# Layer 1's two branches combined sequence by sequence inside the experts' stream, and layer 2's small weights loaded during layer 1

## The chip, the core and the metric

The kernel runs on one core of one Trainium2 chip. Each core has five engines that run on their own and wait for each other through semaphores: TensorE (PE, matmuls; PEld is its weight load), VectorE (DVE), ScalarE (ACT), GpSimd (POOL) and SyncE (SP), which here only issues DMAs. Each engine works through its own list of instructions in order. The metric is device time in microseconds of one launch, the median of three runs.

## The reference, cut to what matters

The input x has 8 sequences of 512 tokens with 128 channels. Four layers follow each other, and each has two branches on the same normalized input, which are multiplied and added to x:

```python
xn = _layernorm(x, axis=-1)
s = _L1_attn_ref(xn, Wq, Wk, Wv, Wo)                  # attention branch of layer 1
g = _silu(_L1_ffn_ref(xn, Wg, W1, b1, W2, b2))        # experts' branch of layer 1
x = x + s * g
xn = _layernorm(x, axis=-1)                           # layer 2 starts from here
s = _L2_attn_ref(xn, ...)
g = _silu(_L2_ffn_ref(xn, ...))
x = x + s * g
```

Layer 1's attention has 16 heads of 8 values with a squared score in place of the exponential. Its second branch is a choice of 8 experts, each of which works on up to 1024 tokens that may belong to any sequence. So `s` of a sequence is known when its attention is done, and `g` of any sequence only when the last expert has added its part.

## The kernel before

Tokens lie 128 to a tile row, so a sequence is `JT` = 4 tiles and all of x is `NT` = 32. x stays on the chip in one tile through all layers.

**Layer 1's loop.** `layer1` (L1133) runs over 128 units (sequence b of 8, group of heads g of 4, block of keys kc of 4). For each unit `weights` (L1065) makes the scores on PE and squares them on ACT (L1078), a mask goes over them on VectorE (L1083), and two units later `sums` (L1088) multiplies them with the values (L1097). `group` (L1105) finishes a group of heads, and after the fourth group of a sequence it makes the attention branch `s` for that sequence (L1128, copied out of PSUM at L120 or L122). One step of the generator `side` is taken per unit: `choice_and_experts` (L963) first picks the tokens of each expert and then runs the eight experts between the attention's instructions.

**The experts' output.** Each expert's result `ys` (L1013, L1014 on VectorE) is added to the array `f_d` in DRAM by eight indirect DMAs that GpSimd issues (L1016). Each of them adds, so each waits for the one before it to land; there are 64 in all.

**Between layers 1 and 2.** When the loop is over, `combine` (L176) takes x in four pieces of two sequences: it loads the piece of `f_d` (L184, SyncE), takes its Silu on ScalarE (L188), multiplies by `s` on VectorE (L189) and adds to x on GpSimd (L194). Then `Layer2` loads its two packs of weights, the small one `c2` (1226 KB) and the large one `f2` (2888 KB), both at L126, and `begin(0)` normalizes the first sequence: sums at L1230, mean at L1231, difference at L1232, squares on ScalarE at L1248, sums of squares at L1250, a power on GpSimd at L1240, product at L1234, and then PE transposes the result (L168). `half_s` (L1270) is layer 2's first reader of `f2`.

**What sets the order.** The order of PE's instructions is the order in which the Python code issues them. That of the other engines' instructions is laid down when the program is built, by a planner that goes by durations of its own; the chip keeps to it. A pool's memory is given to the next pool, and the first writer of the new tile then waits for the last users of the old one.

Of the kernel before, what the change touches and what calls it, by code (L numbers as in the profile page):

```python
# [10 lines left out]
F32 = mybir.dt.float32  # L11
# [3 lines left out]
AF = mybir.ActivationFunctionType  # L15
ALU = mybir.AluOpType
# [4 lines left out]
P = 128  # L21
B = 8
T = 512
C = 128
N = B * T
NT = N // P
JT = T // P
# [8 lines left out]
class Pack:  # L36


    def __init__(self):
        self.parts, self.at, self.n = [], {}, 0  # L40
# [32 lines left out]
def bc(ap, axis, n):  # L73

    a = ap.unsqueeze(axis)
    shape = list(a.shape)
    shape[axis] = n
    return a.to_broadcast(shape)


class Kern:
# [80 lines left out]
    def to_features(self, src, dst, nt=NT, scale=None, bias=None):  # L162

        nc = self.nc
        for g in range(0, nt, 4):
# [6 lines left out]
                nc.vector.tensor_scalar(out, flat, scale, bias, ALU.mult, ALU.add)  # L172
            else:
                self.evac(out, flat)

    def combine(self, pool, x, s, f_dram=None, f=None, x_dram=None):  # L176

        nc = self.nc
        G = 8
        for g in range(0, NT, G):  # L180
            sl = slice(g, g + G)
            if f_dram is not None:
                ft = pool.tile([P, G, C], F32, name="cmb_f")
                nc.sync.dma_start(ft, f_dram[g * P : (g + G) * P, :].rearrange("(j p) c -> p j c", p=P))  # L184
            else:
                ft = f[:, sl, :]
            sg = pool.tile([P, G, C], F32, name="cmb_sg")
            nc.scalar.activation(sg, ft, AF.Silu)  # L188
            nc.vector.tensor_tensor(sg, sg, s[:, sl, :], ALU.mult)  # L189
            old = x[:, sl, :]  # L190
            if x_dram is not None:
                old = pool.tile([P, G, C], F32, name="cmb_x")
                nc.sync.dma_start(old, x_dram[:, sl, :])
            nc.gpsimd.tensor_tensor(x[:, sl, :], old, sg, ALU.add)  # L194

    def causal(self, a, n=None, src=None):

# [720 lines left out]
class Layer1:  # L918
# [4 lines left out]


    def __init__(self, k, cp, x, A, at):
        self.k, self.A = k, A
        nc, tc = k.nc, k.tc
        self.xn_d = k.dram.tile([N, C], F32, name="xn1_d")
        self.f_d = k.f1_d
        self.cn = k.load_consts(cp, A["c1"], at, "c1")  # L930
        self.xT = cp.tile([P, N], F32, name="xT1")
        self.s = cp.tile([P, NT, C], F32, name="s1")
        self.idx = cp.tile([P, E1, 8], I32, name="idx1")
        self.gate = cp.tile([P, E1, 8], F32, name="gate1")

        self.va2 = [cp.tile([P, JT, H * 9 + 23], F32, name=f"va1{i}") for i in range(2)]
        for t in self.va2:
            nc.gpsimd.memset(t, 0.0)
            nc.gpsimd.memset(self.by_head(t)[:, :, :, 8:9], 1.0)


        self.ceiling = cp.tile([P, P], F32, name="ceiling1")
        nc.gpsimd.memset(self.ceiling, float(np.finfo(np.float32).max))
        k.causal(self.ceiling)
        self.sending = False
        with tc.tile_pool(name="l1a", bufs=2) as tp, tc.tile_pool(name="l1a1", bufs=1) as tp1:
            xn = tp1.tile([P, NT, C], F32, name="xn1")
            k.layernorm(tp, x, xn, k.eps5)
            for g in range(0, NT, 8):
                nc.sync.dma_start(  # L950
                    self.xn_d[g * P : (g + 8) * P, :].rearrange("(j p) c -> p j c", p=P), xn[:, g : g + 8, :]
                )
            k.to_features(xn, self.xT)
        self.q = {}
# [8 lines left out]
    def choice_and_experts(self):  # L963

        k, nc, cn, A = self.k, self.k.nc, self.cn, self.A
        idx, gate = self.idx, self.gate
        yield from choose1(k, cn, self.xT, idx, gate)
        self.sending = True
        with k.tc.tile_pool(name="l1w", bufs=2) as wp, k.tc.tile_pool(name="l1e", bufs=2) as ep:
            for e in range(E1):  # L970
                w1 = wp.tile([P, FF1], F32, name="w1_1")
                nc.sync.dma_start(w1, A["w1_1"][:, e * FF1 : (e + 1) * FF1])
                w2 = wp.tile([P, 4, C], F32, name="w2_1")
                nc.sync.dma_start(w2.rearrange("p f c -> p (f c)"), A["w2_1"][:, e * 4 * C : (e + 1) * 4 * C])
                xg = ep.tile([P, 8, C], F32, name="xg1")
                for i in range(8):
                    nc.gpsimd.indirect_dma_start(
                        out=xg[:, i, :], out_offset=None, in_=self.xn_d,
                        in_offset=bass.IndirectOffsetOnAxis(ap=idx[:, e, i : i + 1], axis=0),
                    )  # L980
                if e == 0:
                    yield
                    yield
                xgT = ep.tile([P, 2, 512], F32, name="xgT1")
                for hf in range(2):
                    pt = k.pa((P, 4, P))
                    for i in range(4):
                        nc.tensor.transpose(pt[:, i, :], xg[:, hf * 4 + i, :], k.ident)
                    nc.vector.tensor_copy(xgT[:, hf, :], pt.rearrange("p a b -> p (a b)"))
                yield  # L990
                hT = []
                for hf in range(2):
                    hT.append(ep.tile([P, 4, 512], F32, name="hT1"))
                    for f in range(4):
                        ph = k.pa()
                        nc.tensor.matmul(ph, w1[:, f * P : (f + 1) * P], xgT[:, hf, :], start=True, stop=True)
                        nc.scalar.activation(
                            hT[hf][:, f, :], ph, AF.Gelu, bias=cn["b1"][:, e * 4 + f : e * 4 + f + 1]
                        )
                    yield  # L1000
                ys = ep.tile([P, 8, C], F32, name="ys1", bufs=1)
                for hf in range(2):
                    po = k.pa((P, 4, C))
                    for i in range(4):
                        o = slice(i * P, (i + 1) * P)
                        for f in range(4):
                            nc.tensor.matmul(
                                po[:, i, :], hT[hf][:, f, o], w2[:, f, :], start=(f == 0), stop=(f == 3)
                            )
                        if i == 1:  # L1010
                            yield
                    y = ys[:, hf * 4 : hf * 4 + 4, :]
                    nc.vector.tensor_tensor(y, po, bc(cn["b2"][:, e * C : (e + 1) * C], 1, 4), ALU.add)  # L1013
                    nc.vector.tensor_tensor(y, y, bc(gate[:, e, hf * 4 : hf * 4 + 4], 2, C), ALU.mult)  # L1014
                    for i in range(hf * 4, hf * 4 + 4):
                        nc.gpsimd.indirect_dma_start(  # L1016
                            out=self.f_d, out_offset=bass.IndirectOffsetOnAxis(ap=idx[:, e, i : i + 1], axis=0),
                            in_=ys[:, i, :], in_offset=None, compute_op=ALU.add,
                        )
                    yield  # L1020

    def begin(self, b):

# [81 lines left out]
    def group(self, b, g):  # L1105

        k, nc, cn, yp, q = self.k, self.k.nc, self.cn, self.yp, self.q[b]
# [19 lines left out]
        for j in range(JT):  # L1127
            nc.tensor.matmul(ps[:, j, :], sT[:, j * P : (j + 1) * P], cn["Wo"], start=True, stop=True)  # L1128
        k.evac(self.s[:, b * JT : (b + 1) * JT, :], ps)
        yield  # L1130


def layer1(k, x, A, at):  # L1133
    nc, tc = k.nc, k.tc
    with ExitStack() as ctx:
        ctx.enter_context(k.banks("l1p", pu=2, pf=1, pa=3))
        pool = lambda name, bufs=1: ctx.enter_context(tc.tile_pool(name=name, bufs=bufs))
        L = Layer1(k, pool("l1c"), x, A, at)
# [3 lines left out]
        units = [(b, g, kc) for b in range(B) for g in range(4) for kc in range(JT)]  # L1142
        for _ in L.begin(0):
            pass
        side = L.choice_and_experts()
        held = {}
        front = back = iter(())
        for u in range(len(units) + LAG):
            if u < len(units):
                b, g, kc = units[u]  # L1150
# [11 lines left out]
        for _ in chain(back, side):  # L1162
            pass
        work.close()
        k.combine(pool("l1z", 2), x, L.s, f_dram=L.f_d)

# [89 lines left out]
class Layer2(BySequence):  # L1258


    def __init__(self, k, ctx, x, A, at):
        self.k, self.x = k, x
        nc, tc = k.nc, k.tc
        pool = lambda name, bufs=1: ctx.enter_context(tc.tile_pool(name="l2" + name, bufs=bufs))
        cp = pool("c")
        self.cn = cn = k.load_consts(cp, A["c2"], at[0], "c2")
        self.fn = fn = k.load_consts(cp, A["f2"], at[1], "f2")

        self.half_s = cp.tile([P, 4], F32, name="half_s")
# [260 lines left out]

def layer2(k, x, A, at):

    with ExitStack() as ctx:
        ctx.enter_context(k.banks("l2p", pu=2, pf=1, pa=3))
        L = Layer2(k, ctx, x, A, at)
        units = [(b, g, kc) for b in range(B) for g in range(4) for kc in range(JT)]
# [12 lines left out]
        for u in range(len(units) + LAG):  # L1549
            b, n = divmod(u, U)  # L1550
# [11 lines left out]
            if u >= LAG:  # L1562
                wb, g, kc = units[u - LAG]
# [541 lines left out]

PACKS = (pack0, pack1, pack2, pack3)
LAYERS = (layer0, layer1, layer2, layer3)


# [35 lines left out]
```

## Time and profile before

| | |
|---|---|
| median of three runs | 3640.95 us (3640.08 to 3649.79) |
| the profiled execution's own time | 3647.2 us |
| its span in the profile | 3645.5 us |
| mean granted TensorE clock | 0.83 |
| busy over the span | PE 2815.7 us, DVE 2315.1, ACT 1645.2, POOL 743.0 |
| layer 1's loop ends, last `s` copied | at 1444.6 us |
| PE's first instruction of layer 2 | at 1465.0 us |

A row of the timeline is: start in us, length in us, engine, line, operation, output<-input, shapes, count, and in brackets how long the engine sat idle before it and what ended that. A row with a count above 1 merges neighbours. A row of the table of stretches gives for each stretch the busy time of each engine, the granted TensorE clock as a share of full speed (PEclk), the DMA engines' busy share and the rate. All times of the prediction are those of this one profiled execution, which took 6.25 us more than the median of the runs.

### The profile page before, as it was taken

How to read it: one execution, taken by the hardware profiler on the slowest of the kernel's cores; microseconds unless marked ns; L12 is line 12 of the kernel's file. 1: busy time of each engine (PE TensorE's matmuls, PEld its weight loads, DVE VectorE, ACT ScalarE, POOL GpSimd, SP SyncE). 2: the span in 40 equal slices, each digit the busy share in tenths (PEclk: the TensorE clock that was granted, in tenths of full speed). 3: DMA queues.
4: the chain of work that ended last, by engine and by line, in shares of the span. 5: the costliest groups of instructions: out<-in, count | busy, mean ns of one | idle time of the engine just before them, and what ended most of it. 6: DMA issues, size and time to landing. Idle time of an engine off the chain costs nothing.

```text
span 3645.5 us, 44996 instructions
## 1 busy us (share of the span) xinstructions
PE 2815.7 (77%) x16390; PEld 1512.3 (41%) x16390; DVE 2315.1 (64%) x6346; ACT 1645.2 (45%) x3211; POOL 743.0 (20%) x845
## 2 busy tenths in 40 slices
PE   6173657512998897799999999999678789887987
PEld 4142445302444454344444444443344445444543
DVE  7989898997582334334544544444467777777775
ACT  5162546512544445233333333333245566665665
POOL 0004040400225553101101101101121222222221
PEclk9585757555789999799999999998868889888988
DMA  4003030311002222000000000000000000000000
GB/s 119 2 2 71 1 82 1 72 48 34 1 2 50 41 39 41 42 1 1 1 1 1 1 1 1 1 1 1 21 1 1 4 4 1 4 3 4 1 4 7
DMA packets 67519, 64.53 MB, mean 18 GB/s; under 512 B 5344, under 2 KB 59616, under 8 KB 66784
## 3 DMA queue, kind: packets, MB, share of 16 engines
q1 hardware_dynamic: 39264, 42.75, 3.8%
q0 software_dynamic: 19712, 14.69, 3.1%
q10 hardware_dynamic: 8320, 4.19, 0.4%
q8 instruction: 129, 2.11, 0.2%
q14 instruction: 94, 0.77, 0.1%
HBM read 43.80 MB, written 17.83 MB: 17 GB/s over the span
## 4 chain that ended last, share of the span: by engine, by line
PE 36%; DVE 17%; ACT 7%; POOL 3%; issue 2%; DMA 1%; POOLq 0%; ACTq 0%; DVEq 0%; SPq 0%
PE pa L1372 6%; PE pu L1390 6%; DVE nm L1960 4%; ACT at L1961 3%; PE pu L1957 3%; PE pf L1942 2%; DVE mpad L1404 2%; PE pf L1435 2%; PE pa L1486 1%; PE pa L1485 1%; PE pa L1870 1%; ACT at L1422 1%; PE pa L1915 1%; DVE rope L1863 1%; PE pa L1509 1%
## 5 line engine op out<-in xcount | busy, mean ns | idle before, releaser
L1961 ACT ACTIVATE at<-pu,nm 128x512 f32<-128x512 f32 x512 | 348.1, 688 | 151.6 <-DVE nm L1960 125.1
L1960 DVE TENSOR_REDUCE nm<-pu 128x1 f32<-128x512 f32 x512 | 326.8, 680 | 66.6 <-PE pu L1957 66.5
L199 POOL TENSOR_SCALAR_AFFINE_SELECT at<-at 128x512 f32<-128x512 f32 x184 | 123.3, 670 | 1004.3 <-ACT at L1422 855.9
L1404 DVE TENSOR_REDUCE mpad<-pu 128x2 f32<-128x256 f32 (+3 forms) x256 | 199.2, 818 | 168.6 <-PE pu L1401 168.6
L1422 ACT ACTIVATE at<-pu 128x1024 f32<-128x1024 f32 (+3 forms) x256 | 171.7, 702 | 285.7 <-PE pu L1390 285.5
L1078 ACT ACTIVATE at<-pu,rsqrt 128x1024 f32<-128x1024 f32 (+3 forms) x256 | 190.9, 793 | 190.1 <-PE pu L1073 164.4
L1957 PE MATMUL pu<-qT,kT 32*128 32x512 f32 x1024 | 246.4, 703 | 6.0 <-ACT at L1961 5.1
L1372 PE MATMUL pa<-hid,f 128*128 128x512 f32 x512 | 222.7, 593 | 0.0
L1390 PE MATMUL pu<-qT,kT 32*128 32x512 f32 (+3 forms) x1024 | 160.8, 516 | 56.4 <-DVE mpad L1404 42.0
L748 PE MATMUL pa<-ident,Y 128*128 128x128 f32 x32 | 7.9, 426 | 210.9 <-DVE Y L739 210.9
L1390 PE MATMUL pu<-kT,qT 32*128 32x128 f32 (+3 forms) x1024 | 151.8, 569 | 14.4 <-ACT at L1422 10.2
L1942 PE MATMUL pf<-at,va 128*32 128x512 f32 x1024 | 158.9, 698 | 1.4 <-POOL va L1935 1.4
L548 POOL DMA_INDIRECT xg<-xn_d,idx x48 | 54.9, 1143 | 496.9 <-PE pf L552 316.3
L1372 PEld LDWEIGHTS pa<-hid,f 128*128 128x128 f32 x512 | 96.6, 190 | 119.5 <-issue 118.9
L1493 DVE SCALAR_TENSOR_TENSOR X<-X,u 128x512 f32<-128x512 f32 x56 | 38.7, 691 | 159.5 <-ACT u L1488 159.5
L1073 PE MATMUL pu<-qT,kT 32*128 32x512 f32 (+3 forms) x1024 | 131.1, 518 | 5.7 <-ACT at L1078 4.7
L1390 PEld LDWEIGHTS pu<-qT,kT 32*128 32x128 f32 x1024 | 67.5, 197 | 155.5 <-DVE mpad L1404 116.3
L1016 POOL DMA_INDIRECT f_d<-ys,idx x64 | 103.6, 1619 | 138.0 <-DMA f_d<-ys,idx 86.0
L1935 POOL TENSOR_TENSOR va<-V,sm 128x32 f32<-128x32 f32 x128 | 38.8, 303 | 451.7 <-DVE sm L1934 401.5
L1957 PEld LDWEIGHTS pu<-qT,kT 32*128 32x128 f32 x1024 | 81.9, 209 | 103.2 <-ACT at L1961 65.5
L1373 ACT ACTIVATE hid<-pa,f 128x512 f32<-128x512 f32 x64 | 44.0, 688 | 172.5 <-PE pa L1372 172.5
L1083 DVE TENSOR_TENSOR at<-at,ceiling 128x512 f32<-128x512 f32 x72 | 50.2, 698 | 108.2 <-ACT at L1078 104.8
(611 smaller groups left out, 6723.3 us busy)
## 6 DMA issues: line engine op xcount, KB each, us to landing
w<-in_w_dram SPq DMA_DIRECT2D x24, 512.0 KB, 3.8
f_d<-zeros ACTq DMA_DIRECT2D x8, 512.0 KB
xn_d<-xn SPq DMA_DIRECT2D x8, 512.0 KB, 4.9
w<-in_w_dram SPq DMA_DIRECT2D x16, 256.0 KB, 2.9
w<-in_w_dram SPq DMA_DIRECT2D x24, 128.0 KB
f<-in_f_dram SPq DMA_DIRECT2D x1, 2888.0 KB, 11.8
xn<-in_x_dram SPq DMA_DIRECT2D x4, 512.0 KB, 9.3
Gt<-in_x_dram SPq DMA_DIRECT2D x4, 512.0 KB
```

The costliest lines, as they stand in the source:

```text
L199: self.nc.gpsimd.affine_select(a, a if src is None else src, pattern, ALU.is_ge, 0.0, base=0, channel_multiplier=-1)
L1016: nc.gpsimd.indirect_dma_start(out=self.f_d, out_offset=bass.IndirectOffsetOnAxis(ap=idx[:, e, i : i + 1], axis=0), in_=ys[:, i, :], in_of ...
L1073: nc.tensor.matmul(pu[:, n, 0:m], q["kT"][r, g // 2, kc * P : kc * P + P], q["qT"][r, g, kc * P :], start=True, stop=True,)
L1078: nc.scalar.activation(at_[:, i : i + 2, 0:m], pu[:, :, 0:m], AF.Square, bias=k.rsqrt2, scale=32.0**-0.5)
L1372: nc.tensor.matmul(ps, fn[n][:, c0 : c0 + P], src[:, i, :], start=(i == 0), stop=(i == 3))
L1390: self.k.nc.tensor.matmul(pu[:, n, 0:m], a[r, c0 : c0 + P], b[r, q0 : q0 + m], start=True, stop=stop)
L1404: nc.vector.tensor_reduce(top[:, i : i + 2, 16], pu[:, :, 0:m], AX.X, ALU.max)
L1422: nc.scalar.activation(at_[:, i : i + 2, 0:m], pu[:, :, 0:m], AF.Exp, scale=8.0**-0.5)
L1942: nc.tensor.matmul(po[i * 32 : i * 32 + 32, :], va[:, kc, c0 : c0 + 32], E[:, i, :], start=(kc == 0), stop=(kc == JT - 1))
L1957: nc.tensor.matmul(pu, q["kT"][r, kc * P : (kc + 1) * P], q["qT"][r, g, :], start=True, stop=True)
L1960: nc.vector.tensor_reduce(nm[:, w], pu, AX.X, ALU.max, negate=True)
L1961: nc.scalar.activation(E[:, n, :], pu, AF.Exp, bias=nm[:, w], accum_out=sm[:, w])
```

## The change

`Kern.combine` is removed. `Layer1` gets a generator `combine` of its own that goes over single sequences and is appended to the experts' generator, so that its steps are taken one per unit of the attention loop, after the last expert. A counter `done` tells it how many sequences have their `s`. The add to x moves from GpSimd to VectorE. Pieces become half as large, 128x512 in place of 128x1024, and there are eight of them. `c2` gets a pool of its own, opened before layer 1, and its load is the first thing that `layer1` issues; `Layer2` uses that tile. `f2` is loaded where it was.

```diff
-    def combine(self, pool, x, s, f_dram=None, f=None, x_dram=None):
-        nc = self.nc
-        G = 8
-        for g in range(0, NT, G):
...
-            nc.gpsimd.tensor_tensor(x[:, sl, :], old, sg, ALU.add)
@@ class Layer1
-        self.k, self.A = k, A
+        self.k, self.x, self.A = k, x, A
+        self.done = 0
...
+    def combine(self):
+        k, nc = self.k, self.k.nc
+        with k.tc.tile_pool(name="l1z", bufs=2) as pool:
+            for b in range(B):
+                t = slice(b * JT, (b + 1) * JT)
+                f, g = (pool.tile([P, JT, C], F32, name="cmb_" + n) for n in "fg")
+                nc.sync.dma_start(f, self.f_d[b * T : (b + 1) * T, :].rearrange("(j p) c -> p j c", p=P))
+                nc.scalar.activation(g, f, AF.Silu)
+                while self.done <= b:
+                    yield
+                nc.vector.tensor_tensor(g, g, self.s[:, t, :], ALU.mult)
+                nc.vector.tensor_tensor(self.x[:, t, :], self.x[:, t, :], g, ALU.add)
+                yield
@@ Layer1.group
         k.evac(self.s[:, b * JT : (b + 1) * JT, :], ps)
+        self.done = b + 1
         yield
@@ layer1
+    k.held2 = ExitStack()
+    k.c2 = k.held2.enter_context(tc.tile_pool(name="held2", bufs=1)).tile(list(A["c2"].shape), F32, name="c2")
+    nc.sync.dma_start(k.c2, A["c2"])
...
-        side = L.choice_and_experts()
+        side = chain(L.choice_and_experts(), L.combine())
...
         work.close()
-        k.combine(pool("l1z", 2), x, L.s, f_dram=L.f_d)
@@ Layer2.__init__
-        self.cn = cn = k.load_consts(cp, A["c2"], at[0], "c2")
+        self.cn = cn = Consts(k.c2, at[0])
@@ layer2
-    with ExitStack() as ctx:
+    with k.held2, ExitStack() as ctx:
```

In the changed file the Silu is L1011, the product with `s` L1014, the add to x L1015, the load of a piece of `f_d` L1010 and the load of `c2` L1135. Other lines are given by their numbers before.

More of the change, by code (lines that the diff above doesn't have):

```diff
@@ L174, in to_features @@
                 self.evac(out, flat)
-    def combine(self, pool, x, s, f_dram=None, f=None, x_dram=None):
-        nc = self.nc
-        G = 8
-        for g in range(0, NT, G):
[L181 to L194, printed above, removed]
     def causal(self, a, n=None, src=None):
```

## The prediction

> **What bounds the kernel now.** I read the timeline around the end of layer 1 first, since the change moves work across that border, then the earlier part of the same loop for what a wait on `f_d` does to it, and last the table of stretches for TensorE's clock. The border:
>
> ```profile
> 1438.55 0.66 PE L1111 MATMUL pa<-ident,oT 128*128 128x128 f32 x4 [0.81 <-DVE oT L122]
> 1439.77 7.74 SPq L184 DMA_DIRECT2D cmb_f<-f_d  x4
> 1443.83 1.28 ACT L188 ACT_TABLE_LOAD   x1 [2.06 <-DMA cmb_f<-f_d]
> 1443.93 0.69 DVE L122 COPY s<-pa 128x512 f32<-128x512 f32 x1 [3.84 <-PE pa L1128]
> 1447.58 5.48 POOL L194 TENSOR_TENSOR x<-x,cmb_sg 128x1024 f32<-128x1024 f32 x2 [19.56 <-DVE cmb_sg L189]
> 1454.22 5.68 POOL L194 TENSOR_TENSOR x<-x,cmb_sg 128x1024 f32<-128x1024 f32 x2 [1.16 <-DVE cmb_sg L189]
> 1455.45 1.28 DVE L1230 TENSOR_REDUCE s<-x 128x4 f32<-128x512 f32 x2
> 1459.94 1.29 DVE L1232 TENSOR_TENSOR xn<-x,s 128x512 f32<-128x512 f32 x2 [2.23 <-POOL x L194]
> 1465.07 1.09 PE L168 MATMUL pa<-ident,xn 128*128 128x128 f32 x4 [21.18 <-DVE w L1307]
> ```
>
> Call E the end of the last `s` copy, 1444.6. PE restarts 20.4 us after E: 10.8 go to the combine until VectorE reaches L1230, 4.5 to the sums and a wait for GpSimd's adds, 5.1 to the rest of the normalization. This is what the change is after. But the Silus need `f_d` complete, and that is late:
>
> ```profile
> 1411.29 2.12 ACT L1078 ACTIVATE at<-pu,rsqrt 128x1024 f32<-128x1024 f32 x2 [0.48 <-PE pu L1073]
> 1413.81 1.69 ACT L1078 ACTIVATE at<-pu,rsqrt 128x768 f32<-128x768 f32 x2 [0.40 <-PE pu L1073]
> 1420.16 5.52 ACT L1078 ACTIVATE at<-pu,rsqrt 128x1024 f32<-128x1024 f32 x6 [1.01 <-PE pu L1073]
> 1422.52 1.91 POOL L1016 DMA_INDIRECT f_d<-ys,idx  x1 [2.08 <-DMA f_d<-ys,idx]
> 1426.47 1.56 POOL L1016 DMA_INDIRECT f_d<-ys,idx  x1 [2.03 <-DMA f_d<-ys,idx]
> ```
>
> The experts' arithmetic is over at 1405.1 (the last L1014), but the adds to `f_d` go out one per some 3.7 us, each waiting for the landing of the last; the final one is issued at 1426.5. What happens when an engine's queue meets such a wait is in the trace already:
>
> ```profile
> 1260.78 0.69 DVE L1013 TENSOR_TENSOR ys<-pa,c 128x512 f32<-128x512 f32 x1 [11.82 <-DMA f_d<-ys,idx]
> 1263.11 1.09 PE L168 MATMUL pa<-ident,yb 128*128 128x128 f32 x4 [9.88 <-DVE yb L1119]
> 1264.23 0.59 ACT L120 COPY yT<-pa 128x512 f32<-128x512 f32 x1 [12.90 <-PE pa L168]
> ```
>
> One VectorE instruction waited 11.82 us for `f_d`, and the attention behind it stood still: PE 9.9 us, ACT 12.9. The loop has no store of work that outlives such a wait.
>
> **The change part by part.** (1) *The Silus in the loop.* The order of the built program puts the first two Silus (L1011) on ScalarE directly after the two 128x1024 squares of the last sequence's second group of heads, the row at 1411.29, and before the 128x768 row at 1413.81. Their loads wait for the last add to `f_d`. So ScalarE stands from 1413.4. The last add is issued at 1426.47, takes 1.56 and lands about 2.06 later (the gap between adds): 1430.1. A 256 KB load of 512-byte rows has no row here; the 256 KB weight loads take 2.9 us and the 512 KB `cmb_f` took 4.0 from 1439.8 to 1443.8. I take 3.1: 1433.2. The table load follows the landing, as in the row at 1443.83: 1.28, until 1434.5. Two Silus of 128x512, half of the 1056 ns rows plus some fixed part, 0.63 each: 1435.75. ScalarE resumes 1435.75 - 1413.81 = 21.9 us late. Behind it wait the squares, so VectorE's masks, so PE's `sums`, and PE's next scores for want of a free `pu`.
>
> (2) *The rest of the combine in the loop.* Six more Silus (3.8 us) lie on ScalarE and fourteen products and adds (0.69 each, 9.7 us) on VectorE within four units that took 8.7 us before. I walked the built order from 1435.75 with these durations. The masks of those units each stand behind up to four combine instructions on VectorE. The loads use two buffers, so that Silus 7 and 8 wait for the loads that Silus 5 and 6 released: about 1.1 us more. ScalarE comes to the first 128x768 square of the third group at 1448.9 against 1422.3 (inside the row at 1420.16, after its two 1.06 us squares): 26.6 late; PE's second pair of scores there is 26.0 late. Taking PE, which paces the rest, parts 1 and 2 come to 26.1. The rest of the loop has no slack to give back: over its last three groups the waits alternate between ScalarE and PE, 8.7 us a group.
>
> (3) *The clock after the stall.* The trace:
>
> ```profile
> 1254.00:1256.00 2.00, 0.00 (x0) 0.00 (x0) 0.00 (x0) 0.00 (x0) 1.42 (x2) 1.00 0.41 33
> 1256.00:1258.00 2.00, 0.00 (x0) 0.00 (x0) 0.00 (x0) 0.00 (x0) 1.66 (x2) 0.50 0.25 64
> 1264.00:1266.00 2.00, 2.00 (x9) 0.52 (x8) 0.00 (x0) 0.59 (x1) 0.04 (x1) 0.50 0.37 33
> 1266.00:1268.00 2.00, 2.00 (x20) 1.86 (x17) 0.00 (x0) 1.75 (x2) 1.55 (x1) 0.94 0.00 0
> 1487.00:1490.00 3.00, 1.90 (x14) 0.82 (x8) 1.76 (x2) 0.00 (x0) 0.00 (x0) 0.50 0.00 0
> 1493.00:1496.00 3.00, 3.00 (x6) 1.15 (x6) 1.33 (x2) 0.69 (x1) 0.00 (x0) 0.68 0.00 0
> ```
>
> The clock is halved within 3 us of idling. The Trainium skill ("TensorE: Matmul & The Clock Gate", the HAM clock gate) has it back after one busy window of about 3.4 us; that is 1.7 us of lost PE work, mostly under part 2's VectorE work. The trace agrees at 1263 to 1266, but from 1481 to 1493, where PE was busy for 1.9 to 2.7 of each 3 us, it stayed at 0.50 to 0.55 for 12. Restarted among combine instructions PE is partly busy too. By the rule I would add nothing, by the row up to 4 us. I take 1, nearer to the first, which is the same loop. Sum of the loss: 27.1.
>
> (4) *The border.* After E there remain for the last sequence a product and an add on VectorE (1.4), three 128x1 scalings (0.3), L1230 twice (1.28) and the means (0.35): L1232 starts at E + 3.4, not 15.3. From L1232 to PE it was 5.1 us, so PE starts at E + 8.5. That is 11.9 gained; one 0.68 us sum (L1250) now stands ahead of L172, which may cost 0.3. Gain 11.6. GpSimd's four adds (5.48 + 5.68) vanish; its five memsets (2.8 us) run from about E + 0.9, before its power is wanted at E + 6. On VectorE the adds cost 0.69 each, counted above.
>
> (5) *The loads.* `c2` is issued on SyncE ahead of layer 1's `c1`, at about 882.1, when PE's L758 ends. Even if its 3.5 us (1226 KB at 350 GB/s, less than the 377 to 492 that the table of stretches shows while `c2` and `f2` came in) delayed `c1`, issued at 883.76, in full, `c1` would land by 892, and its first reader is PE's L1032 at 900. Nothing; with that cover gone, up to 3.5. In layer 2, `f2` is issued when the last product is done, E + 0.8, and lands 11.8 us later by its row, E + 12.6, sooner without `c2` beside it. `half_s` stands on VectorE after L172 at about E + 14: no wait; if it were late, L1234 and the queries L1336 would wait behind it, 0 to 2 us. The eight loads of `f_d` block SyncE's queue while they wait, but behind them is only `f2`.
>
> (6) At the border to layer 3, four small VectorE instructions (L1682, L1683, 1.7 us) move from after the last L1519 into a 3.3 us idle gap of VectorE before L1490. L1684 waits for GpSimd's add in either case, which comes 0.6 earlier: gain 0.5, between 0 and 1.5.
>
> Sum: + 27.1 - 11.6 - 0.5 = + 15.0 us. The profiled execution's 3647.2 would become 3662; on the median, 3641 + 15 = 3656, slower by 0.41%. What can be told from no change here is about 0.3%, 11 us.
>
> **The rivals.** *The stall is shorter than the gain (not slower).* If `f_d` is complete earlier, the same program wins. Without any stall, 4.2 of part 2 and 11.6 + 0.5 are left: -8, 3633. The point of balance is a stall of 8 us, that is `f_d` complete by about 1416 rather than 1430. For it: with ScalarE and VectorE standing still GpSimd may issue a little faster (the add at 1415.12 had waited 2.57 rather than 2.06). Against: four adds would have to disappear from a chain whose gaps of 2.03 to 2.10 end with the landing of the add before.
>
> *The loop re-absorbs part (within 0.3%).* Adds faster by 0.7, loads at 2.5, no buffer wait, no cold clock: 15 - 0.7 - 0.6 - 1.1 - 1 = +11 to 12; with a further catch-up between ScalarE and PE +7, 3648. The idle marks of 1.0 us on ScalarE in each group speak for some, PE's 8.2 busy of 8.7 against.
>
> *The clock stays low (more).* PE half-fast for the rest of the loop, as from 1481 to 1493, with `f2` late as well: + 6, 3662.
>
> *The combine is not where the text says.* The built order shows it in the stream for seven sequences, and their Silus before the last two groups; only sequence 8 is after the loop. This can't be.
>
> **How the numbers follow.** The main case, +11 to +19, has 0.62; low clock 0.14; re-absorbed 0.20; not slower by a short stall 0.04. Slower by over 0.3% needs more than +11 and takes nearly all of the first two: 0.75. Same: 0.21, of which the short stall gives 0.02. Faster 0.04, with other unknowns. The range: stall and walk -4 to +4, clock -1 to +3, border 10 to 12.5, runs scattering by some us, so 3646 to 3666, with the upper half of the re-absorbed case.
>
> **What would show it.** In the profile after: ScalarE idle some 20 us before its first L1011, ended by the DMA of `cmb_f`; PE idle almost as long in the loop at a clock falling to 0.5; the last L1128 at about 1470 rather than 1442; PE's gap between L1128 and L168 some 9 us instead of 21; GpSimd without adds to x. Wrong would be: an idle time before L1011 under 10 us, a loop end before 1460, or VectorE waiting for `f2` at L1270.

## The result and the profile after

The changed kernel takes 3658.86 us, the median of six runs (3651.07 to 3663.47), where the kernel before took 3641.64 beside it. The ratio is 1.0033, with a 95% interval of 1.0017 to 1.0049: slower, by 6 to 18 us. Its profiled execution is the quickest of its six (3651.07 us, span 3649.4), so below I compare stretches between marks, not whole spans.

The marks: A is the end of the second 128x1024 square of the last sequence's second group of heads, the last thing ScalarE does before the Silus. E is the end of the last `s` copy, as in the prediction. The border runs from E to PE's first L168 of layer 2. In the changed kernel the scatter is L997, the squares L1074, the load, Silu, product and add of the combine L1010, L1011, L1014, L1015, and Wo's matmul L1124.

The timeline of the changed kernel where the Silus meet `f_d` (start, us, engine, line, what; in brackets the idle time before it and what ended it):

```profile
1404.77 2.12 ACT L1074 ACTIVATE at<-pu,rsqrt 128x1024 f32<-128x1024 f32 x2 [0.48 <-PE pu L1069]
...
1420.11 1.56 POOL L997 DMA_INDIRECT f_d<-ys,idx  x1 [2.01 <-DMA f_d<-ys,idx]
1423.43 14.19 SPq L1010 DMA_DIRECT2D cmb_f<-f_d  x8
1426.28 1.28 ACT L1011 ACT_TABLE_LOAD   x1 [19.39 <-DMA cmb_f<-f_d]
1427.57 1.15 ACT L1011 ACTIVATE cmb_g<-cmb_f 128x512 f32<-128x512 f32 x2
...
1428.63 1.67 ACT L1074 ACTIVATE at<-pu,rsqrt 128x768 f32<-128x768 f32 x2
1429.56 2.02 PE L1069 MATMUL pu<-qT,kT 32*128 32x256 f32 x8 [21.35 <-ACT at L1074]
...
1439.67 0.63 ACT L1011 ACTIVATE cmb_g<-cmb_f 128x512 f32<-128x512 f32 x1 [0.46 <-DMA cmb_f<-f_d]
```

ScalarE ends its squares at 1406.89 (A), then stands 19.39 us for the load of `f_d`. That load cannot go before the last add, issued at 1420.11, has landed. The next square (1428.63) would have begun 0.4 us after A, as in the kernel before; it begins 21.3 us later than that. PE stands 21.35 us behind it. The chain of waits from 1395 to 1480 us puts first the landing of the adds to `f_d`, on which no engine works (share of the time by line, cut at the end):

```profile
by line: DMA f_d<-ys,idx 31.3%; issue 10.7%; PE pu L1069 9.3%; PE pf L1093 7.5%; DMA cmb_f<-f_d 6.6%; ACT at L1074 5.8%; PE pa L1107 3.9%; POOL rs L1240 3.1%; ACT cmb_g L1011 3.0%; PE pa L1124 2.5%; DVE s L1230 2.1%; DVE xn L1234 2.1%; DVE 
```

The border, on the other hand, became what the change aimed at:

```profile
1464.69 0.69 DVE L122 COPY s<-pa 128x512 f32<-128x512 f32 x1 [3.85 <-PE pa L1124]
1466.93 1.27 DVE L1230 TENSOR_REDUCE s<-x 128x4 f32<-128x512 f32 x2
1468.71 1.29 DVE L1232 TENSOR_TENSOR xn<-x,s 128x512 f32<-128x512 f32 x2
1473.73 1.09 PE L168 MATMUL pa<-ident,xn 128*128 128x128 f32 x4 [9.09 <-issue]
...
1482.10 0.16 DVE L1270 TENSOR_SCALAR half_s<-f 128x4 f32<-128x4 f32 x1
```

E is 1465.38 and PE starts at 1473.73: 8.35 us, against 20.4. `half_s` reads `f2` at 1482.10 without a wait. The stretches of all kernels, each from one profiled execution, and the ratio of the times to the kernel before (A and the stretches in us; with two arrays in the loop the Silus stand between the two squares, so that A does not bound them):

| kernel | A | A to E | border | ratio (95%) |
|---|---|---|---|---|
| before | 1413.41 | 31.2 | 20.4 | |
| changed | 1406.89 | 58.5 | 8.3 | 1.0033 (1.0017 to 1.0049) |
| c2 alone | 1413.71 | 31.7 | 21.7 | 0.9989 (0.998 to 0.9998) |
| c2's place alone | 1408.70 | 30.5 | 21.2 | 0.9987 (0.998 to 0.9993) |
| combine after the loop | 1410.09 | 31.1 | 20.6 | 0.9989 (0.9981 to 0.9997) |
| Silus without the wait | 1417.95 | 34.8 | 8.6 | 0.9987 (0.9977 to 0.9998) |
| x by GpSimd | 1411.57 | 58.9 | 9.7 | 1.0029 (1.0018 to 1.0041) |
| Silus held | 1419.04 | 35.6 | 9.0 | 0.9973 (0.9962 to 0.9983) |
| two arrays | - | - | 8.5 | 0.9965 (0.9953 to 0.9977) |
| two arrays, held | 1394.07 | 36.5 | 9.0 | 0.993 (0.9918 to 0.9941) |
| two arrays, held, 4 buffers | 1381.68 | 37.2 | 9.0 | 0.9906 (0.9891 to 0.9922) |
| two arrays, after the loop | 1380.84 | 33.4 | 30.5 | 0.9959 (0.9945 to 0.9973) |

### The profile page after: what moved, and what is told of

It reads as the page before. It is cut to its first block, busy times and chain, and to the rows that moved or that the text cites. A ratio compares the mean times of both kernels' runs of the same rounds, so it can differ in the third digit from the quotient of the medians.

```text
span 3649.4 us, 45022 instructions
## 1 busy us (share of the span) xinstructions
PE 2806.8 (77%) x16390; PEld 1509.2 (41%) x16390; DVE 2316.5 (63%) x6358; ACT 1645.9 (45%) x3215; POOL 735.1 (20%) x841
## 4 chain that ended last, share of the span: by engine, by line
PE 32%; DVE 17%; ACT 7%; POOL 2%; DMA 2%; issue 2%; POOLq 0%; ACTq 0%; DVEq 0%; SPq 0%
PE pa L1372 6%; PE pu L1390 6%; DVE nm L1960 4%; ACT at L1961 4%; PE pu L1957 2%; DVE mpad L1404 2%; DMA f_d<-ys,idx 2%; PE pf L1942 2%; PE pf L1435 2%; PE pa L1486 1%; PE pa L1485 1%; PE pa L1870 1%; ACT at L1422 1%; DVE rope L1863 1%; PE pa L1915 1%
## 5 line engine op out<-in xcount | busy, mean ns | idle before, releaser
L1074 ACT ACTIVATE at<-pu,rsqrt 128x1024 f32<-128x1024 f32 (+3 forms) x256 | 191.0, 792 | 180.7 <-PE pu L1069 150.6
L1957 PE MATMUL pu<-qT,kT 32*128 32x512 f32 x1024 | 246.7, 699 | 6.1 <-ACT at L1961 5.1
L997 POOL DMA_INDIRECT f_d<-ys,idx x64 | 103.6, 1618 | 136.8 <-DMA f_d<-ys,idx 89.9
L1957 PEld LDWEIGHTS pu<-qT,kT 32*128 32x128 f32 x1024 | 82.3, 209 | 103.9 <-ACT at L1961 64.8
```

What stands on the lines that cost most here:

```text
L997: nc.gpsimd.indirect_dma_start(out=self.f_d, out_offset=bass.IndirectOffsetOnAxis(ap=idx[:, e, i : i + 1], axis=0), in_=ys[:, i, :], in_of ...
L1074: nc.scalar.activation(at_[:, i : i + 2, 0:m], pu[:, :, 0:m], AF.Square, bias=k.rsqrt2, scale=32.0**-0.5)
L1957: nc.tensor.matmul(pu, q["kT"][r, kc * P : (kc + 1) * P], q["qT"][r, g, :], start=True, stop=True)
```

## The experiments

**The Silus without the wait.** The combine loads the normalized input, which has long been in DRAM, in place of `f_d`. So the products take other numbers, and x with them; the instructions are the same.

```diff
-                nc.sync.dma_start(f, self.f_d[b * T : (b + 1) * T, :].rearrange("(j p) c -> p j c", p=P))
+                nc.sync.dma_start(f, self.xn_d[b * T : (b + 1) * T, :].rearrange("(j p) c -> p j c", p=P))
```

> The changed kernel, but the combine loads its pieces from the array of layer 1's normalized input in place of the experts' output, so the Silu is taken of other numbers and no load waits for the experts' adds. Measured from the second 128x1024 square of the last sequence's second group of heads to the end of the last copy of s: 31.2 us before, 58.5 us in the changed kernel. Stall theory (ScalarE's queue waits for the array): no idle time of over 3 us in front of a Silu, the stretch 32 to 37 us, the gap from the last copy of s to TensorE's first transpose of layer 2 about 8.4 us as in the changed kernel (20.4 before), total about 8 us under before (3633). Load theory (the products, adds and Silus are themselves too much work for the loop): stretch 45 us or more, total above before.

Its timeline, the first and the last Silu:

```profile
1403.57 1.28 ACT L1011 ACT_TABLE_LOAD   x1 [0.68 <-DMA cmb_f<-xn_d]
...
1420.03 0.63 ACT L1011 ACTIVATE cmb_g<-cmb_f 128x512 f32<-128x512 f32 x1 [1.56 <-DMA cmb_f<-xn_d]
```

No wait before a Silu is longer than 1.56 us. The stretch A to E falls from 58.5 to 34.8 us with the same combine instructions, and the border stays at 8.6. But the planner put the Silus one group earlier here, six of the eight ahead of A, so 34.8 leaves out most of the combine. From the same square one group earlier to E it is 41.6 us in the kernel before, 68.8 in the changed kernel and 52.0 here. So 16.8 of the 27.3 us lost are the wait, and at this place the combine still costs 10.4. That uses up nearly all of the 12 us of the border. The time is 4.7 us below that of the kernel before (ratio 0.9987), less than the 8 expected, and `c2` alone, below, gives about as much. The wait is the larger part of what the loop lost, not all of it.

**The Silus held.** The same combine on the real `f_d`, but a Silu may not start before the last sequence's third group of heads is done: it takes a bias of zero that VectorE makes from that group's output. Eight load buffers let the loads go ahead, and the combine's steps are taken from unit 127 on.

```diff
+        if (b, g) == (B - 1, 2):
+            nc.vector.tensor_scalar(self.late, oT[:, 0:1], 0.0, None, ALU.mult)
...
-                f, g = (pool.tile([P, JT, C], F32, name="cmb_" + n) for n in "fg")
+                f, g = (pool.tile([P, JT, C], F32, name="cmb_" + n, bufs=w) for n, w in (("f", 8), ("g", 2)))
...
-                nc.scalar.activation(g, f, AF.Silu)
+                nc.scalar.activation(g, f, AF.Silu, bias=self.late)
...
-        side = chain(L.choice_and_experts(), L.combine())
+        side, late = L.choice_and_experts(), L.combine()
...
+            if u >= 127:
+                next(late, None)
```

> The changed kernel with the Silus held back: they take a bias of zero that VectorE makes from the output of the last sequence's third group, so that their place on ScalarE falls after the adds have landed; eight load buffers in place of two. Stall theory: ScalarE waits less than 3 us for a load, the stretch from the second 128x1024 square to the last copy of s is 32 to 36 us, the gap to layer 2's first transpose 9 to 10 us, total 6 to 10 us under before (about 3633). Load theory: the same work squeezed into half the units makes the stretch 40 us or more, total no better than before.

Its timeline:

```profile
1416.92 2.12 ACT L1075 ACTIVATE at<-pu,rsqrt 128x1024 f32<-128x1024 f32 x2 [0.48 <-PE pu L1070]
1419.43 1.69 ACT L1075 ACTIVATE at<-pu,rsqrt 128x768 f32<-128x768 f32 x2 [0.40 <-PE pu L1070]
...
1439.60 1.28 ACT L1012 ACT_TABLE_LOAD   x1
...
1446.43 1.33 ACT L1012 ACTIVATE cmb_g<-cmb_f,late 128x512 f32<-128x512 f32 x2 [1.69 <-DVE x L1016]
```

The squares run through after A. The table load of the first Silu comes at 1439.60 without a wait; the last add to `f_d` had gone out at 1431.82. A to E is 35.6, the border 9.0, and the kernel is faster than the kernel before and than the changed one (ratio 0.9973). The combine's work, on the same engines, gains or loses by where its wait stands in ScalarE's queue. What is left against the kernel before, 4.4 us in A to E, is the combine itself, and it is 4.4 from one group earlier too (45.9 against 41.6); the prediction had 4.2 for it.

**The combine after the loop.** The changed kernel, its combine run when the loop is over.

```diff
-        side = chain(L.choice_and_experts(), L.combine())
+        side = L.choice_and_experts()
...
+        for _ in L.combine():
+            pass
```

> The changed kernel with its own combine run after the loop and not in the experts' stream: eight half-size pieces, adds on VectorE, c2 loaded during layer 1. Stall theory: stretch in the loop 31 us as before, gap to layer 2 about 20 us (two load buffers make four pairs of about 3.6 us each, against GpSimd's slow adds before), total within 2 us of before. Theory that the adds on VectorE and the half-size pieces or the early c2 cost the time: 10 us or more above before.

A to E is 31.1 and the border 20.6: both as before the change. The time is some 4 us below the kernel before, where at most 2 were expected; `c2` alone, below, has the same ratio. The new form of the combine (pieces by sequence, x by VectorE) gains nothing at the border; its place in the loop makes both the 12 us of gain and the 27 of loss.

**x by GpSimd.** The changed kernel with the adds to x given back to GpSimd, still in the stream.

```diff
-                nc.vector.tensor_tensor(self.x[:, t, :], self.x[:, t, :], g, ALU.add)
+                nc.gpsimd.tensor_tensor(self.x[:, t, :], self.x[:, t, :], g, ALU.add)
```

> The changed kernel with one engine exchanged: the adds to x stay in the experts' stream, but GpSimd makes them, as before. Stall theory (the first Silu waits on ScalarE for the end of the chain of adds to f_d, and the squares wait behind it): nothing changes at the stall; ScalarE idle about 20 us in front of the first Silu, from the second 128x1024 square of the last group but two to the last s copy 55 to 59 us (58.5 in the changed kernel), the border from the last s copy to the first transpose of layer 2 longer by up to 2 us (GpSimd's add takes about 2 us for VectorE's 0.69, and one of them is last), time about +15 to +17 us on the kernel before, ratio 1.004 to 1.005. The rival, that VectorE's six or eight more instructions in the loop slow it: the stretch falls by 5 us or more, and the time comes to within 10 us of the kernel before, ratio 1.002 or less.

Its timeline:

```profile
1409.45 2.12 ACT L1074 ACTIVATE at<-pu,rsqrt 128x1024 f32<-128x1024 f32 x2 [0.48 <-PE pu L1069]
1429.69 1.28 ACT L1011 ACT_TABLE_LOAD   x1 [18.12 <-DMA cmb_f<-f_d]
...
1432.04 1.67 ACT L1074 ACTIVATE at<-pu,rsqrt 128x768 f32<-128x768 f32 x2
```

The stall is the same, A to E 58.9, and the ratio of 1.0029, under the 1.004 to 1.005 expected, cannot be told from the changed kernel's 1.0033. That VectorE's adds to x slow the loop is refuted; the part of the change that moves x to VectorE is worth 1.4 us at the border (9.7 against 8.3).

**c2 alone.** The kernel before with a place of its own for `c2` and its load at layer 1's start.

```diff
+    k.held2 = ExitStack()
+    k.c2 = k.held2.enter_context(tc.tile_pool(name="held2", bufs=1)).tile(list(A["c2"].shape), F32, name="c2")
+    nc.sync.dma_start(k.c2, A["c2"])
...
-        self.cn = cn = k.load_consts(cp, A["c2"], at[0], "c2")
+        self.cn = cn = Consts(k.c2, at[0])
```

> The kernel before with only c2's load moved to the start of layer 1 and to a place of its own. Stall theory: no effect in layer 1 (c1's first reader comes 16 us after its issue), at the border 0 to 1 us gained, total -1 to +1 us. Placement theory (the load ahead of c1, or the moved tiles, slow layer 1): 5 us or more above before, seen between the load of c1 and the first square of layer 1's loop.

A ratio of 0.9989, some 4 us of gain, where nothing was expected; and A to E and the border are no shorter than before.

**c2's place alone.** As above, with the line of the load moved back to layer 2.

```diff
-    nc.sync.dma_start(k.c2, A["c2"])
...
+        nc.sync.dma_start(k.c2, A["c2"])
         self.cn = cn = Consts(k.c2, at[0])
```

> The kernel before with a place of its own for c2, the load left where it was, at layer 2's start. The earlier run with place and early load had ratio 0.9989 (0.998 to 0.9998), where nothing was expected. If that gain is the early load, this one has ratio 1.000 within 0.001; if it is the place (the load no longer waits for layer 1's buffers, or lies elsewhere), 0.998 to 0.9995 again; if it was chance, both are 1.000.

The gain is there again (0.9987). But this run does not separate place from early load: with a buffer that nobody else uses, the planner sent the load off at 882.53 us all the same. So it is in effect a second run of c2 alone, and says that the gain is no chance.

The traces say where it lies: in layer 3, behind the border of term (6). VectorE there, in the kernel before and in the changed one:

```profile
2627.36 0.69 DVE L1519 TENSOR_TENSOR xn<-xn,pa 128x512 f32<-128x512 f32 x1 [9.41 <-PE pa L1515]
2627.96 0.68 DVE L1682 TENSOR_REDUCE s<-x 128x4 f32<-128x512 f32 x1
2628.56 0.68 DVE L1525 SCALAR_TENSOR_TENSOR th<-th,xn 128x512 f32<-128x512 f32 x1
...
2630.62 0.69 DVE L1684 TENSOR_TENSOR xn<-x,s 128x512 f32<-128x512 f32 x1 [0.71 <-POOL x L1527]
```

```profile
2637.85 0.69 DVE L1519 TENSOR_TENSOR xn<-xn,pa 128x512 f32<-128x512 f32 x1 [9.40 <-PE pa L1515]
2638.57 0.69 DVE L1525 SCALAR_TENSOR_TENSOR th<-th,xn 128x512 f32<-128x512 f32 x1
2640.64 0.69 DVE L1684 TENSOR_TENSOR xn<-x,s 128x512 f32<-128x512 f32 x1 [1.38 <-POOL x L1527]
```

From the last L1519 to the first L1684 it takes 3.26 us before and 2.79 after, since no sum (L1682) stands ahead of L1525 any more: 0.47 us gained, as predicted. From that L1684 to the end the kernel before takes 1014.9 us, the changed kernel 1008.8, which is far more. Two rows of PE's timeline of the kernel before, and its table of stretches (start and end, length, busy us of PE, PEld, DVE, ACT, POOL, then the granted TensorE clock):

```profile
2692.89 1.14 PE L1957 MATMUL pu<-qT,kT 32*128 32x512 f32 x8
2697.02 2.93 PE L1957 MATMUL pu<-qT,kT 32*128 32x512 f32 x8
```

```profile
2696.00:2699.00 3.00, 3.00 (x19) 1.46 (x12) 2.61 (x7) 2.34 (x7) 0.00 (x0) 1.00 0.00 0
2699.00:2702.00 3.00, 3.00 (x13) 2.24 (x13) 2.96 (x5) 2.00 (x6) 0.24 (x1) 0.64 0.00 0
2702.00:2705.00 3.00, 3.00 (x14) 2.67 (x13) 2.23 (x4) 1.05 (x4) 1.29 (x1) 0.50 0.00 0
2705.00:2708.00 3.00, 3.00 (x16) 1.95 (x16) 1.84 (x5) 0.74 (x2) 1.09 (x2) 0.50 0.00 0
2708.00:2711.00 3.00, 3.00 (x22) 2.04 (x14) 1.49 (x5) 0.00 (x0) 0.00 (x0) 0.65 0.00 0
```

The same stretch of the changed kernel, where it comes some 10 us later, and of the kernel with c2's place alone:

```profile
2707.31 2.83 PE L1957 MATMUL pu<-qT,kT 32*128 32x512 f32 x8
```

```profile
2709.00:2712.00 3.00, 3.00 (x21) 2.23 (x20) 3.00 (x6) 2.00 (x6) 0.24 (x1) 1.00 0.00 0
2712.00:2715.00 3.00, 3.00 (x22) 1.90 (x22) 2.44 (x9) 1.87 (x6) 2.37 (x2) 1.00 0.00 0
```

```profile
2693.40:2703.40 10.00, 10.00 (x65) 7.02 (x63) 9.05 (x22) 5.78 (x17) 2.70 (x4) 1.00 0.00 0
```

In the kernel before, TensorE's clock falls to a half for about 10 us; over the four rows from 2699 on, that is 3 x 0.36 + 3 x 0.5 + 3 x 0.5 + 3 x 0.35 = 5.1 us of lost PE time. In the others it stays at 1.00. The 3.00 us of PE just ahead of the fall is not full work: the eight matmuls of L1957 took 1.14 us at 2692.89, and at 2697.02 they are strung over 2.93 us, their weight loads waiting three times for ScalarE. A row counts this as busy because the ends of matmuls are modelled. But the same thin stretch is in the changed kernel (2.83 us) and in the ten others (2.80 to 2.83), and there the clock holds.

What differs is how the work lies against the clock. Measured from the last L1519, the clock's first fall comes after 4.1 to 4.2 us in all twelve traces. L1684, and layer 3 behind it, comes after 3.26 us in the kernel before and after 2.8 in the eleven others, which all load `c2` early. With ScalarE's instructions of layer 3 in the same order in all twelve, none of the eleven is ahead of the kernel before 61 us after L1684, and each is 5.2 to 5.3 us ahead after 91: most of the 6.1 us comes from this one fall of the clock, which none of them has. So the 0.47 us of the border seem to become 5 us through the clock. This is argued from the traces, one of each kernel, and not shown: a direct test would need the phase alone changed, and it was not tried.

**Two arrays.** The cause of the late landing halved: the adds of an expert go by turns to two DRAM arrays, so that an add waits for the one before the last. The combine loads both, and GpSimd adds them.

```diff
+            k.f1b_d = k.dram.tile([N, C], F32, name="f1b_d")
+            k.zero_dram(tp, k.f1b_d, zeros)
...
-                            out=self.f_d, out_offset=bass.IndirectOffsetOnAxis(ap=idx[:, e, i : i + 1], axis=0),
+                            out=(self.f_d, self.k.f1b_d)[i % 2], out_offset=bass.IndirectOffsetOnAxis(ap=idx[:, e, i : i + 1], axis=0),
...
+                nc.sync.dma_start(h, k.f1b_d[b * T : (b + 1) * T, :].rearrange("(j p) c -> p j c", p=P))
+                nc.gpsimd.tensor_tensor(f, f, h, ALU.add)
```

> The changed kernel with the cause of the late landing shortened: a sequence's experts' adds go by turns to two arrays in DRAM, so that each add waits for the one before the last; the combine loads both and GpSimd adds them (8 loads and 8 adds more, one array more to set to zero in layer 0). Stall theory: adds come every 1.9 to 2.2 us in place of 3.6, the last one lands 10 to 20 us earlier against the squares, ScalarE's idle time in front of the first Silu falls from 19.4 us to 0 to 8, the stretch from the second 128x1024 square to the last s copy from 58.5 to 33 to 45 us, the border stays at 8 to 10 us, and VectorE's waits for the ys buffer (40 us in six waits in the experts' stream) shrink to under 15. Time -8 to -25 us on the kernel before, ratio 0.993 to 0.998. A rival, that the adds are limited by the DMA queue or by GpSimd's issue and not by the order on one array: adds stay 3.3 us apart or more, the stall stays over 15 us, ratio 1.003 or more.

Its timeline:

```profile
1387.39 1.55 POOL L999 DMA_INDIRECT f1b_d<-ys,idx  x1 [0.30 <-issue]
1389.68 1.55 POOL L999 DMA_INDIRECT f_d<-ys,idx  x1 [0.74 <-DMA f_d<-ys,idx]
1391.54 1.55 POOL L999 DMA_INDIRECT f1b_d<-ys,idx  x1 [0.31 <-issue]
...
1391.43 1.11 ACT L1078 ACTIVATE at<-pu,rsqrt 128x1024 f32<-128x1024 f32 x1 [0.48 <-PE pu L1073]
1395.49 1.28 ACT L1015 ACT_TABLE_LOAD   x1 [2.95 <-DMA f1b_d<-ys,idx]
1401.11 0.63 ACT L1015 ACTIVATE cmb_g<-cmb_f 128x512 f32<-128x512 f32 x1 [4.33 <-POOL cmb_f L1014]
1402.51 0.63 ACT L1015 ACTIVATE cmb_g<-cmb_f 128x512 f32<-128x512 f32 x1 [0.77 <-POOL cmb_f L1014]
```

Adds go out every 1.9 to 2.3 us, so their rate was set by the order on one array and not by the queue or the issue. The idle time before the first Silu is 2.95 + 4.33 us and the ratio 0.9965, both as expected. But my expectation for the loop failed in substance. From the second square to E it is 45.0 us, at the edge of the 33 to 45 expected, but only because the first waits now stand ahead of that square. From the first of the two 128x1024 squares (its end, 1392.5) to E it takes 56.6 us; the same stretch is 59.6 in the changed kernel and 37.6 with two arrays and held Silus. The Silus still stand among the squares, and seven of the eight now wait for GpSimd's sum. The gain came from elsewhere, as the next two show.

**Two arrays, held.** Both edits together.

> Both remedies: two arrays for the adds, and the Silus held back by a bias that VectorE makes in the last sequence's third head group. If the stall is the only loss of the stream and the hold already takes it away, two arrays add only what VectorE's waits for the ys buffer cost the loop: 0 to 15 us on the held kernel, which had ratio 0.9973; expected 0.993 to 0.997. If those waits cost the loop nothing, the eight added loads and adds are seen alone: 0.997 to 0.999. No idle time of ScalarE over 3 us in front of a Silu by either.

VectorE's waits for the `ys` buffer, in the changed kernel (line waited for, us, times, longest):

```profile
DVE ys L994 <- DMA f_d<-ys,idx: 40.2, 6, 11.7
```

With two arrays that line is gone. The held kernel goes from 0.9973 to 0.993 through it, 0.43% or some 16 us, at the upper end of what was expected. A to E is 36.5, near that with one array (35.6), and A comes earlier. The whole is 3617.5 us (3616.01 to 3623.48).

**Two arrays, after the loop.** The two arrays with the combine behind the loop, so that no Silu is in it.

> Two arrays for the adds, with the combine run after the loop: no Silu stands in the loop. It tells what two arrays give to the loop by themselves, through VectorE's waits for the ys buffer. If these waits held the loop back, the second 128x1024 square of the last group but two ends near 1394 us, as it did with two arrays and held Silus (1414 to 1419 with one array), the border from the last s copy to the first transposes is 20 to 25 us, and the time -14 to -22 us: ratio 0.994 to 0.996. If the gain came only with the held Silus (from a stall that was left in the held kernel), the loop ends as with one array and the ratio is 0.998 to 1.000.

Ratio 0.9959, as expected. The border is 30.5 us, 10 more than with one array and above the 20 to 25 expected, since every Silu now waits for GpSimd's sum (line waited for, us, times, longest):

```profile
ACT cmb_g L1015 <- POOL cmb_f L1014: 18.1, 8, 4.4
```

The loop has gained all the same: 0.3% better than the combine after the loop with one array (0.9989) in spite of 10 us at the border, so about 20 us. The two arrays help the loop by themselves, through `ys`, and not through the stall.

**Two arrays, held, 4 buffers.** Four buffers in place of two for the Silus' outputs.

```diff
-(("f", 8), ("g", 2))
+(("f", 8), ("g", 4))
```

> The kernel with two arrays and held Silus (ratio 0.993), with four buffers for the Silus' outputs in place of two. There ScalarE stood 1.41, 1.69 and 2.15 us in front of later Silus till VectorE had added the buffer's last content to x, with the last squares' way to the last s copy behind it. If these waits are on the path, they go and the time falls by 2 to 5 us: ratio 0.9915 to 0.9925 if the kernel before comes out the same. If they lie beside other waits of the loop's tail, nothing: 0.9925 to 0.9935.

The best kernel: 3604.53 us (3597.82 to 3606.55), ratio 0.9906. But the waits that the edit was to take away stayed in its profile (0.17, 1.68 and 2.15 us), so the expectation fell with them. The profile shows the difference to the kernel with two buffers in another place, the passage from the choice to the experts; first two buffers, then four:

```profile
1090.00:1150.00 60.00, 49.60 (x394) 21.73 (x387) 21.24 (x41) 26.66 (x39) 29.86 (x33) 0.89 0.16 49
```

```profile
1090.00:1150.00 60.00, 55.18 (x513) 27.43 (x505) 27.63 (x52) 33.03 (x46) 31.09 (x34) 0.97 0.18 49
```

PE is busy 55.18 of 60 us rather than 49.60. The edit changes no order of instructions there. The kernel with two arrays and the combine after the loop, run beside it, has the busier form too (55.66), and its A, 1380.84, is as early as the one here, 1381.68, where two buffers had 1394.07. So the difference lies ahead of A, where the edit does nothing. What sets them stays open. The two intervals overlap (0.9891 to 0.9922 and 0.9918 to 0.9941), and I credit the edit with nothing.

## Why the prediction was right

The time came out as said: 3656 predicted, in a range of 3646 to 3666, and 3658.86 measured. The mechanism did too: the stall, what it costs and what the border gives back. That the total lies so near is in part luck, as (6) shows.

**The Silus in the loop (1).** Predicted 21.9 us late, measured 21.3. The load took 2.85 from its issue, which the last add's landing released, to the table load (3.1 predicted, no row for it), the table load 1.28 and two Silus 1.15 together. The run without the wait and the held one, which take 16.8 and 22.9 of the 27.3 us away, show that the stall is the cause and not only beside it.

**The rest of the combine (2) and the clock (3).** Loss from A to E predicted 27.1, measured 58.5 - 31.2 = 27.3. Inside it two terms were off in opposite senses. The wait for the two load buffers was 0.46 and not 1.1. And the clock did not come back as the rule that I leaned to would have it:

```profile
1422.00:1425.00 3.00, 0.00 (x0) 0.00 (x0) 0.00 (x0) 0.00 (x0) 0.00 (x0) 0.50 0.35 50
...
1434.00:1437.00 3.00, 3.00 (x23) 1.21 (x25) 1.74 (x5) 1.67 (x4) 0.00 (x0) 0.50 0.38 114
1437.00:1440.00 3.00, 2.30 (x20) 0.57 (x16) 3.00 (x7) 1.65 (x3) 0.00 (x0) 0.97 0.58 175
1440.00:1443.00 3.00, 1.78 (x18) 0.76 (x16) 2.42 (x5) 3.00 (x5) 0.00 (x0) 1.00 0.02 5
1443.00:1446.00 3.00, 2.91 (x16) 0.50 (x13) 1.77 (x3) 1.78 (x3) 0.00 (x0) 0.66 0.00 0
1446.00:1449.00 3.00, 3.00 (x30) 1.90 (x28) 1.16 (x5) 0.84 (x2) 0.00 (x0) 0.77 0.00 0
```

PE restarts at 1429.56 and has the full clock only from about 1437, 7.6 us later, where the Trainium skill ("TensorE: Matmul & The Clock Gate", the HAM clock gate) asks for at least one busy window of about 3.4 us, which I had taken for exactly one. After PE was busy for only 1.78 of 3 us (1440 to 1443) the clock fell again. The row that I weighed against the rule, a clock that stays low under partial work, was the better guide. The low clock up to 1437 seems to have cost little beside VectorE's combine: counted from A, ScalarE comes to the first 128x768 square of the third group (1441.72) 25.9 us later than before, and the walk without any clock had 26.6, of which 1.2 were too much for the stall and the buffers. Another 1.3 us were lost behind that square, where the clock was at 0.66 and 0.77; the prediction had 1 for the clock in all. No run separates the clock from the rest.

**The border (4).** Predicted 8.5 us and a gain of 11.6; measured 8.35 and 12.1. With the combine after the loop the gain is not there.

**The loads (5).** `half_s` had no wait, as said. That an early `c2` is worth nothing was right for this border: with c2 alone it is no shorter.

**The border to layer 3 (6).** Predicted 0.5 us, measured 0.47 at the border itself. But what followed was missed: layer 3 as a whole took 6.1 us less, 5.1 of it the clock's fall that is missing. I had not looked at the clock beyond layer 2's start. With it the sum is + 27.3 - 12.1 - 6.1 = + 9 rather than + 15, inside the interval of the ratio (6 to 18 us). The two profiled executions differ by only 3.9 us: A came 6.5 us earlier in the changed kernel, and layer 2 took 1.4 longer. Ahead of A nothing of the combine runs in these two, and A lay anywhere from 1406.9 to 1419.0 us in the seven kernels with one array of which that holds, so I take the 6.5 for scatter. That is also why the loop ended at 1465 and not at about 1470. The medians of the first comparison lie 17 us apart, within the interval but well above the + 9; so the 3658.86 owes some of its nearness to 3656 to scatter.

**The rivals.** A stall shorter than the gain did not come in this kernel; the held kernel is that rival made, and its ratio of 0.9973, 10 us below the kernel before, is near the - 8 worked out for it, though `c2` alone gives some 4 of the 10. The loop took nothing back: 6.0 us were lost after the stall, and 5.2 predicted.

## What to carry to other kernels

Work moved from a border into a loop carries its waits along: look in the trace for when its last input lands and what stands behind it on the in-order engine, and place it after that point; here the same Silus cost 27 us ahead of the landing and 4 behind it. When a chain of accumulating transfers to one array is what lands late, split the array: the chain halves, and what waited for its buffers elsewhere in the loop goes with it. A change far from a stretch can move it against the clock's steps and so change its time by several microseconds; compare the granted clock of every layer before giving a small gain a reason.

## What the hardware showed that was not expected

A shift of half a microsecond that seems to decide over a fall of the clock: in layer 3 of the kernel before TensorE ran at 0.50 for about 10 us (5.1 us lost) after a stretch in which eight matmuls that take 1.14 us were strung over 2.93; in the eleven other traces layer 3 lies 0.4 to 0.5 us earlier against the clock, the same stretch is there, and the clock held. A slow restart: 7.6 us at 0.50 after PE went to work again behind the stall. Chained indirect adds to one DRAM array go out 3.5 to 4.1 us apart (1.56 of issue and about 2 till the landing), and 1.9 to 2.3 apart on two arrays.
